# Two pre-activation convolutions by row transforms: an image's last outer products into their own slot, layer 2's statistics one slot earlier

## The chip, the cores and the metric

The kernel runs on one core of a Trainium2 chip. The metric is the device time of one execution in microseconds (us); of several executions the median is given. Below, TensorE is PE in the profile, VectorE is DVE, ScalarE is ACT, GpSimd is POOL, and SyncE is SP. A "q" behind an engine's name (SPq) marks its instructions that issue transfers. All data are float32. Time before: 1962.35 us, the median of three executions (1960.58 to 1964.09).

## What is computed

```python
# x: (8, 32, 252, 252); two weights: (32, 32, 5, 5)
def _gn(v, G=16, eps=1e-5):
    B_, C_, H_, W_ = v.shape
    g = v.reshape(B_, G, C_ // G, H_, W_)
    m = jnp.mean(g, axis=(2, 3, 4), keepdims=True)
    s = jnp.var(g, axis=(2, 3, 4), keepdims=True)
    return ((g - m) / jnp.sqrt(s + eps)).reshape(v.shape)

x = x + _L0_conv_ref(_gn(x), L0_conv_weight)    # 5x5, padded by reflection, written with FFTs
x = x + _L1_conv_ref(_gn(x), L1_conv_weight)
```

Each layer normalises every image in 16 groups of two channels over all its pixels, convolves it with a 5x5 filter whose border is reflected, and adds the input. A layer's normalisation needs sums over the whole image, so layer 2 of an image can't start before the last row of its layer 1 has its sums.

## The kernel before

**Layout.** 32 channels, the parity of a row and the parity of a column together fill the 128 partitions; so an image is 126 x 126 positions, and the 5x5 filter becomes a 3x3 one between 128-wide vectors. The normalisation is put into the weights (the scale) and into a bias (the mean), and the addition of the input into the weights too, by an identity block. In the code layer 1 has `l = 0` and layer 2 `l = 1`.

**Tiling.** Both layers cut each image into eight chunks `c` of 16 rows (four tiles `t` of four output rows). Rows are transformed so that four output rows take six products, called points 0 to 5, each of three matmuls (one per column of the filter) of 504 or 508 columns. VectorE makes the transformed inputs: row differences `v` (L544, and L546 for the last rows, which need the next chunk), quad terms `u12` (L554 to L557), then `t24` for points 2 and 4 (L565, L569), `t13` for 1 and 3 (L575, L572), `t05` for 0 and 5 (L582).

**A slot** is one chunk of one layer. The list `order` alternates layer 1 of image b+1 with layer 2 of image b; the first eight slots are layer 1 of image 0, the last eight layer 2 of image 7. In a slot TensorE computes points 2 and 4 into the banks `m2` and `m4`. ScalarE copies each into `pairs1` and `pairs3` as a "seed" (L691, L693) on which points 1 and 3 are then accumulated, and keeps a copy in `sd` (L699). VectorE combines them into the two middle output rows (L710, L718, L719).

The "outer" points 0 and 5, which make rows 0 and 3 of each tile, come in one of three ways:

- late (the usual one): in the following slot, accumulated on sums in the bank pair `sums05`, which ScalarE reads out (L734);
- by columns (`by_columns`): smaller products on column sums `sdiff`, `d`, half in the own slot in `extra` with a seed by ScalarE (L674), the rest in the next in `sums05`, read out by L746;
- at once (the set `at_once`): in the own slot, into `extra`, added and read out by VectorE (`outer`, L732).

**Statistics.** Reading out also gives row sums; ScalarE squares each finished chunk of layer 1 (`squares`, L818). When chunk 7 is in, `finish_stats` runs a chain for layer 2: `moments` on VectorE (`tot`, `mv`, `dk`, `nvar`), `group_mean` (a small matmul, L337), `deviations` (VectorE), `group_var` (a small matmul, L358), `variance` (VectorE's `var`, L364, then ScalarE's root `std`, L366), `inverse` (VectorE, to `rstd`). Then ScalarE scales the weights `u` (L506) and GpSimd adds the identity blocks (L474). The weights come from a copy in device memory (`ud`), written once by ScalarE's queue and fetched for each image by SP. Layer 1's own statistics of the next image are sums over 14 pieces `st` of x, read by SP and summed on ScalarE (L228, L230, L234).

For the early chunks of images 0 and 1, x is loaded only once and the second half of the partitions is made on the chip: GpSimd fills borders (L145 to L148) and ScalarE copies the even columns (`even_columns`, L156).

**What sets the order.** Nothing is scheduled by a planner: each operation is put into a table with a planned time by `at(t, fn, ...)`, the table is sorted, and every engine executes its own instructions in that order. The planned times decide the order alone; what waits in practice is decided by semaphores. `begin(i)` is the planned start of slot i. `t0`, `t1`, `t2` are the starts of a slot and of the next two. SP's transfers stand in one line in the same way.

The end of image b's layer 1 and the start of its layer 2, with the slots (b, l, c) = (b, 0, 7), (b-1, 1, 7), (b+1, 0, 0), (b, 1, 0), is called the boundary of image b below.

Of the kernel before, what the change touches and what calls it, by code (L numbers as in the profile page):

```python
# [42 lines left out]
ALU = mybir.AluOpType  # L43
# [10 lines left out]
def tile_conv_preact_x2(ctx: ExitStack, tc: tile.TileContext, x: bass.AP, w0: bass.AP, w1: bass.AP, out: bass.AP):  # L54
# [34 lines left out]
    def at(t: float, fn, *args, **kw):  # L89
        table.append((t, len(table), fn, args, kw))  # L90
# [437 lines left out]
    def transform(t0: float, t1: float, b: int, l: int, c: int, free: float = -100.0, now=(0, 0, 0)):  # L528
# [10 lines left out]
        def row_pairs(j0: int = 0, j1: int = NT):  # L539
            if j0 == 0:  # L540
                got["v"] = vpool.tile([P, ROWS, wi], F32, tag="v", name=f"v_{b}_{l}_{c}")
            v, (t, nxt) = got["v"], source()
            r0, r1 = 4 * j0, min(4 * j1, ROWS - 2)
            V.tensor_sub(v[:, r0:r1], t[:, r0 + 2 : r1 + 2], t[:, r0:r1])  # L544
            if j1 == NT:
                V.tensor_sub(v[:, r1:ROWS], nxt[:, 0:2], t[:, r1:ROWS])  # L546
            got["vt"] = v.rearrange("p (t i) w -> p t i w", i=4)

        def row_quads(j0: int = 0, j1: int = NT):
            if j0 == 0:  # L550
                got["u"] = vpool.tile([P, 2, NT, wi], F32, tag="u12", name=f"u12_{b}_{l}_{c}")
            u1, u2, (t, nxt) = got["u"][:, 0], got["u"][:, 1], source()
            r0, k1 = 4 * j0, min(j1, NT - 1)
            stt(u1[:, j0:j1], t[:, r0 + 1 : 4 * j1 : 4], -4.0, t[:, r0 + 3 : 4 * j1 : 4], ALU.mult, ALU.add)  # L554
            stt(u2[:, j0:k1], t[:, r0 + 2 : 4 * k1 : 4], -4.0, t[:, r0 + 4 : 4 * k1 + 1 : 4], ALU.mult, ALU.add)
            if j1 == NT:
                stt(u2[:, k1], t[:, ROWS - 2], -4.0, nxt[:, 0], ALU.mult, ALU.add)  # L557

        def point2(j0: int = 0, j1: int = NT):
            if j0 == 0:  # L560
# [43 lines left out]
        if (b, l, c) == order[0]:  # L604
            at(t0 - 33.3, row_quads, 0, 2)
            at(t0 - 31, point2, 0, 2)
            for fn in (row_pairs, point4):
                at(t0, fn, 0, 2)
            for fn in (row_quads, point2, row_pairs, point4):
                at(t0 + 0.2, fn, 2, 4)  # L610
            at(t0 + 4.9, point1)
            at(t0 + 5.5, point3)
            at(t0 + 6.2, points05)
        else:
            for dt, fn in ((0, row_pairs), (2, row_quads), (3.6, point2), (4.2, point4)):
                at(t0 + dt, fn)
            at(max(t0 + 5.5, free + 7.8), point1)
            at(max(t0 + 5.6, free + (11.1 if by_columns(*now) else 10.25)), point3)
            at(t1, points05)
            if by_columns(b, l, c):  # L620
                at(t1 + 1.5, columns)


    def conv(b: int, l: int, c: int, t0: float, t1: float, t2: float = 0.0, j0: int = 0, j1: int = NT, m05=None, later: float = 10.2):
# [130 lines left out]
            V.tensor_sub(half(sums05, 1, both, no), odd, m12[:, :, :, 0:no])  # L755

        step = 2.55 * f
        for i, k in enumerate((2, 4, 1, 3)):
            for h in range(3):
                if first and i < 2:  # L760
                    for j in (0, 2):
                        at(t0 + 1.3 * i + step * j / 2 + 0.1 * h, product, k, h, j, j + 2)
                else:
                    at(t0 + step * (i + h / 3) + (0.85 if columns and i == 3 and h else 0.0), product, k, h)
        for i, k in enumerate(() if columns else (0, 5)):
            for h in range(3):
                at((t1 - 2 * step if m05 else t1 + later) + step * (i + h / 3), product, k, h)
        for e in range(2):
            t = t0 + (5.1 * f if e else 3.9 if first else 2.6 * f)
            at(t, seed, e)  # L770
# [5 lines left out]
        if columns:  # L776
            for i in range(4):
                at(t0 + (11.05 if i % 2 else 8.5) + 0.2 * i, column_product, 2 - i % 2, i // 2)
                at(t1 + later + 0.4 * i, column_product, 3 * (i % 2), i // 2)
            at(t0 + 9.3, seed_columns)  # L780
            at(t0 + 12.9, parts05)
            at(t1 + 1.5, column_parts)
            for i in range(2):
                at(t2 + 0.05, outer_columns, i)
        elif m05:
            at(t0 + 12.9 * f, parts05)
            if (b, c) == (0, NCH - 1) or (l == 1 and nt == NT):
                at(t1 - 0.01, open_rest)
            at(t1, outer, 0)
            at(t1, outer, 1)  # L790
        else:
            at(t1 + 1.5, parts05)
            at(t2 + 0.05, outer, 0)
            at(t2 + 0.05, outer, 1)
        if nt < NT:
            store_half(t1, b, c, j0 // 2, got)
        elif l == 0:
            keep(t1, None if m05 else t2, b, c, got)
        else:
            store(t1 + 1.5 if m05 else t2 + 0.7, b, c, got)  # L800


    def keep(t1: float, t2, b: int, c: int, got):
# [33 lines left out]
            at(t1 + (0.4 if t2 is None else 2.0), shift)  # L837
        last = c == NCH - 1
        if t2 is None:
            times = t1 + 0.5, t1 + (8.7 if last else 13.4), t1 + 6.6  # L840
        else:
            times = t1 + 13.5, t2 + (0.7 if last else 9.7), t2 + 7.8
        if (b, c) == (0, 0):
            times = t1 + 5.9, *times[1:]
        at(times[0], squares, 0, slice(0, NT), slice(1, 3))
# [67 lines left out]

    at_once = {order.index(n) for n in [(0, 0, c) for c in range(NCH)] + [(0, 1, 0), (B - 2, 1, NCH - 3)]}

    def by_columns(b: int, l: int, c: int) -> bool:
        if l == 0:
# [6 lines left out]
    def begin(i: int) -> float:  # L926

        return sum(10.2 + (own + [0.0])[j] + (late[j - 1] if j else 0.0) for j in range(i))


    chained = {order.index((b, 0, NCH - 1)) + 2 for b in range(B)}


    t0 = -100.0
# [53 lines left out]
    for i, (b, l, c) in enumerate(order):  # L988
# [9 lines left out]
        else:  # L998
            conv(b, l, c, t0, t1, t2, later=10.2 + own[i + 1])
        if i + 1 < len(order):  # L1000
            transform(t0 + (6.3 if i == 0 else 3.5 if i in chained else 2.9), t1 + 0.2, *order[i + 1], free=t0, now=(b, l, c))
            nb, nl, ncx = order[i + 1]
            k = inputs.index((nb, ncx)) + 2
            if nl == 0 and 2 < k < len(inputs):
                for part in parts(*inputs[k]):
                    at(t0 + (14.0 if nb == 0 and part[0] == ROWS else 4.0), load, *inputs[k], *part)
                    at(t1 + 0.2, borders, *inputs[k], *part)
                    if once(*inputs[k]):
                        at(t1 + (0.3 if part[0] == 0 else 8.5), even_columns, *inputs[k], *part)
        if c == 0 and any(by_columns(b, l, k) for k in range(NCH)):  # L1010
            t = begin(i - 1) if l == 0 and b > 1 else t1 if l == 0 else t0
            at(t + 5.4, halve_middle, b, l)
# [4 lines left out]
        if l == 0 and b + 1 < B:  # L1017
            wide = 1 if b == 0 else 2
            if c == 0:
                for j in range(2):  # L1020
                    at(begin(i - 1 if b > 1 else i) + 1.0, load_piece, b + 1, j)
            if c < NPIECE // 2:
                for j in range(2):
                    p = 2 * c + j
                    t = (t1 if wide == 2 and j else t0) + (8.6 + 2.5 * j if wide == 1 else 9.8)
                    at(t, piece_sums, b + 1, p)
                    if p + 2 < NPIECE:
                        at(t + 2.6, load_piece, b + 1, p + 2)
# [5 lines left out]
                    at(t0 + (9.5, 10.4, 11.3)[j], scale_points, b + 1, 0, ks)  # L1034
                    at(t0 + (10.4, 12.3, 14)[j], lambda b=b, ks=ks: add_residual(G, scaled[b + 1, 0], ks))
        if l == 0 and c == NCH - 1:
            at(t2 + 0.1, fetch_weights, b, 1)
            finish_stats(b, 1, *(t2 + t for t in (1.45 if b else 0.1, 3.41, 3.42, 6.85, 7.0, 7.6)))
            for j, ks in enumerate(pairs):
                at(t2 + (9.5, 10.4, 13.6)[j], scale_points, b, 1, ks)  # L1040
                at(t2 + (10.4, 12.4, 14.5)[j], lambda b=b, ks=ks: add_residual(G, scaled[b, 1], ks))

    with tc.manual_schedule(engines={E.PE, E.DVE, E.Activation, E.Pool, E.SP}):
        for _, _, fn, args, kw in sorted(table, key=lambda e: e[:2]):
# [33 lines left out]
```

## Time and profile before

| | |
|---|---|
| median of three executions | 1962.35 us (1960.58 to 1964.09) |
| the profiled execution | 1960.66 us |
| its span, first to last instruction | 1958.9 us |
| TensorE busy, mean granted clock | 1894.1 us (97%), 0.988 |
| VectorE busy | 1749.5 us (89%) |
| ScalarE busy | 1400.0 us (71%) |
| GpSimd busy | 235.9 us (12%) |
| moved by DMA | 276.09 MB, 141 GB/s on average |

The page gives each engine's busy time, the chain of work that ended last, and the costliest groups. The table of waits gives, for one engine, the instruction that waited, what released it, the total, how often and the longest. A timeline gives single instructions (or runs of equal ones): start, duration, engine, line, operation, output and input, how many records, and in brackets the idle time before them with what ended it. A matmul of 504 columns has two records. The windows give the busy time of each engine in a stretch, the granted clock of TensorE, and the DMA's share.

### The profile page before, as it was taken

Reading aid. Unit: us, or ns where it says so; the run is one execution under the profiler, and the core shown is the slowest. Engines: PE = TensorE matmul, PEld = TensorE weight load, DVE = VectorE, ACT = ScalarE, POOL = GpSimd, SP = SyncE. Lnnn points to the kernel's source line nnn. Section 1 sums busy time; section 2 is a strip of 40 time slices with the busy share of each in tenths; the row PEclk is TensorE's granted clock in tenths of the full one; section 3 lists DMA queues with packets and bytes.
Section 4 is the critical chain, followed back from the end, with each engine's and each line's share of the span. In section 5 each row is a group of like instructions: output and inputs, shape, how many; then the busy total and the mean of one; then the engine's idle time right before and its main releaser. Section 6 shows DMA issues by size and latency. Waiting matters only on the chain.

```text
span 1958.9 us, 19376 instructions
## 1 busy us (share of the span) xinstructions
PE 1894.1 (97%) x5068; PEld 947.7 (48%) x5068; DVE 1749.5 (89%) x2924; ACT 1400.0 (71%) x2703; POOL 235.9 (12%) x541
## 2 busy tenths in 40 slices
PE   5999999999999999999999999999999999999998
PEld 4444444444544444544544444444454445444445
DVE  7978899899989999989989999989989999988896
ACT  5866677777777777777777687776877765665575
POOL 3542000110001100011000210002000020000100
PEclk8999999999999999999999999999999999999999
DMA  9875465757765766756856757666767636541133
GB/s 271 202 163 148 107 156 141 160 125 171 163 142 126 167 157 146 168 122 151 182 131 141 168 120 182 138 144 149 149 161 165 139 88 124 113 100 50 41 78 89
DMA packets 220974, 276.09 MB, mean 141 GB/s; under 512 B 16448, under 2 KB 204224, under 8 KB 218688
## 3 DMA queue, kind: packets, MB, share of 16 engines
q1 hardware_dynamic: 220384, 272.09, 61.5%
q10 hardware_dynamic: 480, 2.77, 0.4%
q8 instruction: 40, 0.66, 0.2%
q14 instruction: 70, 0.57, 0.1%
HBM read 207.41 MB, written 67.39 MB: 140 GB/s over the span
## 4 chain that ended last, share of the span: by engine, by line
PE 87%; DVE 5%; ACT 3%; DMA 3%; POOL 1%; issue 1%; SPq 0%; ACTq 0%; POOLq 0%; DVEq 0%
PE pairs L648 31%; PE m L648 30%; PE sums L648 15%; PE sums L670 5%; PE extra L670 5%; PE extra L648 2%; DMA st<-in_x_dram 1%; DVE v L544 1%; POOL u L474 1%; DMA xs<-in_x_dram 1%; ACT junk L818 1%; DMA wraw<-in_L_conv_weight_dram 0%; ACT y L734 0%; DVE d L595 0%; ACT u L506 0%
## 5 line engine op out<-in xcount | busy, mean ns | idle before, releaser
L648 PE MATMUL pairs<-t,u 128*128 128x504 f32 (+2 forms) x1548 | 690.5, 587 | 7.9 <-ACT pairs L691 4.5
L648 PE MATMUL m<-t,u 128*128 128x508 f32 (+3 forms) x1560 | 679.2, 583 | 5.0 <-POOL u L474 2.5
L648 PEld LDWEIGHTS pairs<-t,u 128*128 128x128 f32 x1548 | 291.4, 190 | 341.6 <-issue 322.9
L648 PEld LDWEIGHTS m<-t,u 128*128 128x128 f32 x1560 | 294.5, 190 | 330.3 <-issue 315.3
L875 ACT COPY o<-y 64x508 f32<-64x508 f32 x496 | 326.6, 659 | 9.4 <-DVE y L732 1.0
L648 PE MATMUL sums<-t,u 128*128 128x508 f32 (+3 forms) x732 | 314.8, 577 | 0.0
L734 ACT ACTIVATE y<-sums 128x508 f32<-128x508 f32 (+2 forms) x120 | 64.6, 583 | 218.7 <-PE sums L648 218.7
L582 DVE SCALAR_TENSOR_TENSOR t<-v 128x1024 f32<-128x1024 f32 (+1 forms) x128 | 157.8, 1233 | 60.8 <-PE sums L648 60.1
L648 PEld LDWEIGHTS sums<-t,u 128*128 128x128 f32 x732 | 137.8, 189 | 146.0 <-issue 139.0
L710 DVE SCALAR_TENSOR_TENSOR sd<-sd,pairs 128x504 f32<-128x504 f32 (+2 forms) x258 | 166.8, 672 | 43.1 <-PE pairs L648 41.2
L145 POOL COPY xs<-xs 64x32 f32<-64x32 f32 (+3 forms) x74 | 38.7, 523 | 1115.9 <-DMA xs<-in_x_dram 811.2
L699 ACT COPY sd<-m 128x504 f32<-128x504 f32 (+2 forms) x258 | 149.9, 581 | 1.5
L818 ACT ACTIVATE junk<-y,negk 128x1008 bf16<-128x1008 f32 x144 | 148.3, 1030 | 2.5
L706 ACT COPY sd<-pairs 128x504 f32<-128x504 f32 (+1 forms) x129 | 74.1, 574 | 88.2 <-PE pairs L648 84.2
L670 PE MATMUL extra<-sdiff,wc 128*128 128x252 f32 (+2 forms) x456 | 115.6, 375 | 20.8 <-ACT extra L674 20.8
L544 DVE TENSOR_TENSOR v<-xs 128x1792 f32<-128x1792 f32 (+1 forms) x65 | 129.9, 1999 | 0.7
L544 DVE TENSOR_TENSOR v<-y 128x1806 f32<-128x1806 f32 x64 | 130.0, 2031 | 0.0
L693 ACT COPY pairs<-m 128x504 f32<-128x504 f32 (+1 forms) x129 | 72.8, 564 | 75.0 <-PE m L648 73.3
L670 PEld LDWEIGHTS extra<-sdiff,wc 128*128 128x128 f32 x456 | 85.5, 190 | 82.3 <-issue 48.4
L234 ACT ACTIVATE st<-st,negk 128x1134 f32<-128x1134 f32 x98 | 121.7, 1242 | 3.3
L228 ACT ACTIVATE st<-st 128x1134 f32<-128x1134 f32 x98 | 112.0, 1143 | 4.4 <-DMA st<-in_x_dram 3.3
L670 PE MATMUL sums<-d,u 128*128 128x252 f32 (+2 forms) x456 | 108.4, 380 | 0.0
(172 smaller groups left out, 2221.9 us busy)
## 6 DMA issues: line engine op xcount, KB each, us to landing
xs<-in_x_dram SPq DMA_DIRECT2D x176, 504.0 KB, 8.5
st<-in_x_dram SPq DMA_DIRECT2D x111, 567.0 KB, 4.4
out_dram<-o SPq DMA_DIRECT2D x488, 126.0 KB, 6.7
u<-ud SPq DMA_DIRECT2D x15, 1152.0 KB, 6.1
xs<-in_x_dram SPq DMA_DIRECT2D x30, 441.0 KB, 6.8
xs<-in_x_dram SPq DMA_DIRECT2D x28, 472.5 KB, 8.3
ud<-uraw ACTq DMA_DIRECT2D x2, 1152.0 KB, 7.5
xtail<-in_x_dram SPq DMA_DIRECT2D x64, 31.5 KB, 6.4
```

The costliest lines, as they stand in the source:

```text
L228: A.activation(junk, src, AF.Identity, accum_out=acc[:, 0, i : i + 1])
L234: A.activation(junk, src, AF.Square, bias=negk, accum_out=acc[:, 1, i : i + 1])
L544: V.tensor_sub(v[:, r0:r1], t[:, r0 + 2 : r1 + 2], t[:, r0:r1])
L582: stt(t, got["vt"][:, :, 0:2], -4.0, got["vt"][:, :, 2:4], ALU.mult, ALU.add)
L648: T.matmul(dst, u[:, k, 2 - i, :], rhs[:, j0 + i0 : j0 + i1, i : i + wo], start=(i == 0 and not add), stop=(i == 2), skip_group_check=add,)
L670: T.matmul(dst[:, 0, use], w, rhs[:, use], start=(i == 2), stop=True, skip_group_check=(i != 2))
L693: A.copy(dst, src)
L699: A.copy(got["sd"][:, 1 + e], m24[e][:, 0:n])
L706: A.copy(got["sd"][:, 0], pairs13[0][:, 0:n])
L710: stt(d, d, -2.0, pairs13[e][:, 0:n], ALU.mult, ALU.add)
L818: A.activation(dst, src, AF.Square, bias=negk, accum_out=acc[:, 1, at_ : at_ + 1])
L875: copy(got["o", h][halves[s], 0:m, cp::2], got["y"][halves[cp], r : r + m, :])
```

## The change

- The last chunk of layer 1 of images 1 to 7, (b, 0, 7), joins the set `at_once`; image 0's was in it already. Its outer products go into `extra` in its own slot and are read out by VectorE. `open_rest` (one small identity matmul on the rest of `extra`) now follows in each of these slots.
- In such a slot the own outer products come directly after the inner ones, ahead of the late ones of the slot before: they are placed by `te`, which is `t0 + 6 * step`, and no more by the start of the next slot.
- Layer 2's chain of statistics, the fetch of its weights, their scaling and their residual are placed from `te = t0 + 15.3`, where they were placed from `t2`, two slots on. The squares of chunk 7 are placed earlier, its reflection copies later (`te + 22`).
- `last_rows` takes the last rows of `v` and `u12`, which need the next chunk, out of `row_pairs` and `row_quads`, and stands after both.
- The copies of even columns of the first two rows of a chunk come at `t1 + 5.25` instead of `t1 + 0.3`; both parts of (1, 0) at other times too.
- The first two loads of pieces of image 2, and the sums of the first piece, come later; the set `chained`, which put one transform per image 0.6 later, goes.

```diff
         def row_pairs(j0: int = 0, j1: int = NT):
...
             V.tensor_sub(v[:, r0:r1], t[:, r0 + 2 : r1 + 2], t[:, r0:r1])
-            if j1 == NT:
-                V.tensor_sub(v[:, r1:ROWS], nxt[:, 0:2], t[:, r1:ROWS])
...
         def row_quads(j0: int = 0, j1: int = NT):
...
-            if j1 == NT:
-                stt(u2[:, k1], t[:, ROWS - 2], -4.0, nxt[:, 0], ALU.mult, ALU.add)
+
+        def last_rows():
+
+            v, u2, (t, nxt) = got["v"], got["u"][:, 1], source()
+            V.tensor_sub(v[:, ROWS - 2 : ROWS], nxt[:, 0:2], t[:, ROWS - 2 : ROWS])
+            stt(u2[:, NT - 1], t[:, ROWS - 2], -4.0, nxt[:, 0], ALU.mult, ALU.add)
...
-            for dt, fn in ((0, row_pairs), (2, row_quads), (3.6, point2), (4.2, point4)):
+            for dt, fn in ((0, row_pairs), (2, row_quads), (3.2, last_rows), (3.6, point2), (4.2, point4)):
                 at(t0 + dt, fn)
...
         step = 2.55 * f
+        te = t0 + 6 * step if nt == NT else t1
...
-                at((t1 - 2 * step if m05 else t1 + later) + step * (i + h / 3), product, k, h)
+                at((te - 2 * step if m05 else t1 + later) + step * (i + h / 3), product, k, h)
...
         elif m05:
             at(t0 + 12.9 * f, parts05)
-            if (b, c) == (0, NCH - 1) or (l == 1 and nt == NT):
-                at(t1 - 0.01, open_rest)
-            at(t1, outer, 0)
-            at(t1, outer, 1)
+            if c == NCH - 1 if l == 0 else nt == NT:
+                at(te - 0.01, open_rest)
+            at(te, outer, 0)
+            at(te, outer, 1)
...
-            keep(t1, None if m05 else t2, b, c, got)
+            keep(te if m05 else t1, None if m05 else t2, b, c, got)
...
         if t2 is None:
-            times = t1 + 0.5, t1 + (8.7 if last else 13.4), t1 + 6.6
+            times = (t1 - 1.9, t1 + 1.6, t1 + 22) if last else (t1 + 0.5, t1 + 13.4, t1 + 6.6)
         else:
-            times = t1 + 13.5, t2 + (0.7 if last else 9.7), t2 + 7.8
+            times = t1 + 13.5, t2 + (0.7 if b == B - 1 and c == NCH - 2 else 9.7), t2 + 7.8
...
-    at_once = {order.index(n) for n in [(0, 0, c) for c in range(NCH)] + [(0, 1, 0), (B - 2, 1, NCH - 3)]}
+    at_once = {order.index(n) for n in [(0, 0, c) for c in range(NCH)] + [(b, 0, NCH - 1) for b in range(B)] + [(0, 1, 0), (B - 2, 1, NCH - 3)]}
...
-    chained = {order.index((b, 0, NCH - 1)) + 2 for b in range(B)}
...
-            transform(t0 + (6.3 if i == 0 else 3.5 if i in chained else 2.9), t1 + 0.2, *order[i + 1], free=t0, now=(b, l, c))
+            transform(t0 + (6.3 if i == 0 else 2.9), t1 + 0.2, *order[i + 1], free=t0, now=(b, l, c))
...
                     if once(*inputs[k]):
-                        at(t1 + (0.3 if part[0] == 0 else 8.5), even_columns, *inputs[k], *part)
+                        kb, kc = inputs[k]
+                        t = 5.25 if part[0] == 0 and (kb, kc) != (1, 0) else 13.55 if kb else 8.5
+                        at(t1 + t, even_columns, *inputs[k], *part)
...
             if c == 0:
                 for j in range(2):
-                    at(begin(i - 1 if b > 1 else i) + 1.0, load_piece, b + 1, j)
+                    at(begin(i - 1) + 1.0 if b > 1 else t0 + (8.0 if b else 1.0), load_piece, b + 1, j)
             if c < NPIECE // 2:
                 for j in range(2):
                     p = 2 * c + j
-                    t = (t1 if wide == 2 and j else t0) + (8.6 + 2.5 * j if wide == 1 else 9.8)
+                    t = (t1 if wide == 2 and j else t0) + (8.6 + 2.5 * j if wide == 1 else 14.5 if (b, p) == (1, 0) else 9.8)
                     at(t, piece_sums, b + 1, p)
...
         if l == 0 and c == NCH - 1:
-            at(t2 + 0.1, fetch_weights, b, 1)
-            finish_stats(b, 1, *(t2 + t for t in (1.45 if b else 0.1, 3.41, 3.42, 6.85, 7.0, 7.6)))
+            te = t0 + 15.3
+            at(te + 0.1, fetch_weights, b, 1)
+            finish_stats(b, 1, *(te + t for t in (3.0 if b < B - 1 else 4.4, 6.85, 6.86, 10.25 if b else 9.9, 12.82, 13.55)))
             for j, ks in enumerate(pairs):
-                at(t2 + (9.5, 10.4, 13.6)[j], scale_points, b, 1, ks)
-                at(t2 + (10.4, 12.4, 14.5)[j], lambda b=b, ks=ks: add_residual(G, scaled[b, 1], ks))
+                at(te + (14.5, 15.5, 21)[j], scale_points, b, 1, ks)
+                at(te + (15.5, 17.5, 22)[j], lambda b=b, ks=ks: add_residual(G, scaled[b, 1], ks))
```

## The prediction

> **What bounds the kernel now.** I read the page first, for busy shares and the chain that ended last, and then the table of TensorE's waits.
>
> ```profile
> PE 1894.1 (97%) x5068; PEld 947.7 (48%) x5068; DVE 1749.5 (89%) x2924; ACT 1400.0 (71%) x2703; POOL 235.9 (12%) x541
> ...
> PE 87%; DVE 5%; ACT 3%; DMA 3%; POOL 1%; issue 1%; SPq 0%; ACTq 0%; POOLq 0%; DVEq 0%
> ```
> ```profile
> PE extra L670 <- ACT extra L674: 20.8, 7, 3.0
> ...
> PE pairs L648 <- ACT pairs L691: 4.5, 4, 3.1
> PE m L358 <- DVE sq L352: 3.8, 6, 0.6
> PE pairs L648 <- issue: 3.3, 1, 3.3
> PE m L648 <- POOL u L474: 2.5, 3, 0.8
> ```
>
> TensorE sets the time. No matmul is removed, so only its waits can be won. They sum to 55.8 us; 19.7 lie in the start (the statistics' first load, 14.9, and five small ones). The other 36.1 are spread: 20.8 are seven waits of 3.0, one per image, for ScalarE's seed of `extra`; the rest stand beside them or in image 0. Half-speed stretches follow: six, at 136.7, 174.3, 658.9, 894.5, 1604.4 and 1822.9 us. Summing what matmuls took above their steady spacing (0.845 for 504 columns) over each boundary gives 14.1 in image 0 (100 to 300 us) and 5.3, 5.8, 5.8, 5.4, 5.3, 4.9, 5.2 in images 1 to 7. In all about 46, of which 10 is the clock.
>
> Next the timelines around image 1's boundary: ScalarE, VectorE, TensorE.
>
> ```profile
> 412.05 0.59 ACT L699 COPY sd<-m 128x504 f32<-128x504 f32 x1
> 418.33 0.20 ACT L366 ACTIVATE std<-var 128x1 f32<-128x1 f32 x1 [5.70 <-DVE var L364]
> ...
> 420.85 0.56 ACT L674 ACTIVATE extra<-extra 128x504 f32<-128x504 f32 x1
> ```
> ```profile
> 414.58 2.04 DVE L544 TENSOR_TENSOR v<-y 128x1806 f32<-128x1806 f32 x1
> ...
> 418.15 0.15 DVE L364 TENSOR_SCALAR var<-m 128x1 f32<-128x1 f32 x1
> ```
> ```profile
> 421.47 1.01 PE L670 MATMUL extra<-sdiff,wc 128*128 128x189 f32 x4 [2.98 <-ACT extra L674]
> ```
>
> ScalarE stands 5.70 us before the square root of layer 2's variance, since VectorE does 3.6 us of `v` and `u12` before `var`. Behind the root queue a copy, eight reflection copies (2.1) and the seed, which TensorE wants at 418.5. So the chain of statistics, placed in the slot in which `extra` is needed, makes the stall.
>
> The same engine's windows show what is left to win from:
>
> ```profile
> 411.90:427.20 15.30, 10.86 (x36) 5.91 (x35) 14.40 (x31) 9.42 (x23) 4.16 (x9) 1.00 0.43 133
> ...
> 442.50:457.80 15.30, 15.30 (x42) 7.53 (x41) 15.16 (x25) 10.66 (x24) 1.32 (x2) 1.00 0.66 169
> ```
>
> The columns are length, then PE, PEld, DVE, ACT and POOL. VectorE is busy 14.40 of the 15.30 in which TensorE stalls, and 15.16 two slots later. It has hardly any slack there.
>
> Image 0 has stalls of another kind (ScalarE, then SP's DMA issues):
>
> ```profile
> 172.48 0.42 ACT L156 COPY xs<-xs 64x256 f32<-64x256 f32 x1 [6.46 <-POOL xs L148]
> ...
> 174.06 0.63 ACT L691 ACTIVATE pairs<-m,means 128x504 f32<-128x504 f32 x1
> ```
> ```profile
> 160.52 0.94 SPq L247 DMA_DIRECT2D st<-in_x_dram  x2
> 174.70 2.02 SPq L140 DMA_DIRECT2D xs<-in_x_dram  x4
> 176.83 0.47 SPq L467 DMA_DIRECT2D u<-ud  x1
> ```
>
> A copy of even columns, waiting 6.46 for GpSimd's borders, stands before the seed; TensorE idles 3.26 until 174.79. The same happens at 137.71 (3.13).
>
> [...] The stretches here begin right after waits of 3.0 to 3.3, and granted clock in the slice at 656.7 to 672.0 is 0.89, some 1.7 us lost in 15.3. At images 1, 4 and 5 the same wait is followed by no such stretch, but by the 0.8 for GpSimd's `u`, so it depends on phase. [...] In 158 to 173 us 469 GB/s is the most the trace shows, and about 190 while strided image rows load (178 to 184).
>
> **The change part by part, images 1 to 6.** I walked image 1 (slot (1,0,7) starts at 373.99 in both).
>
> 1. Outer products of chunk 7: six matmuls (3 x 0.845 + 3 x 0.634 = 4.44) move one slot forward. TensorE's sum: 0, plus one identity matmul (about 0.14, the price of the small ones before). They end at 389.2 and the identity at 389.4. ScalarE loses two evacuations (0.59 + 0.48), VectorE gains two (0.60 + 0.48).
> 2. The chain. On VectorE: outer ends 390.8; `tot` waits for ScalarE's last squares until 391.9 (idle 1.15), `nvar` 392.8. Then `t05` (1.2) and the column forms (2.5) to 396.6; `mean` waits for TensorE's small matmul, 397.4 (0.8 idle). `v` and its followers for (2,0,0) take to 402.5, `var` 403.2. ScalarE's root follows; the seed of `extra` is ready at about 405.5 where TensorE wants it at 405.8: the 2.98, the 0.64, the 0.82 and the clock go, 5.3 to 5.8. What hides the wait for `var` is 0.3 us of slack; if `var` is later, the seed is late by as much.
> 3. What is late next. VectorE has done 1.1 us more and idled 2, so its lead grows by one us only. After `rstd` (406.1) it has 9.8 of differences, sums and outer rows, then `v` of (1,1,0) at 415.9 and 4.2 for `t24`: ready 420.1, wanted at 419.65, since TensorE comes 4 us sooner. I get stalls of 0.5 there, 1.0 at (2,0,1) and 0.5 a slot on, 2.0 to 2.2 with the identity. Gain per boundary 5.4 - 2.1 = 3.3; six make 19.8. From both sides: 5.4 if VectorE is never late, 1 if it is late by one us more in each of two slots.
> 4. Later squares, reflection and weights: the reflection copies (2.1) leave the critical stretch; they are read more than ten slots on, and ScalarE has 4 us of slack a slot (71% busy). The fetch of `u` moves a slot ahead on SP, past the statistics' loads of image b+2; it waits for the buffer until about 389, and those loads are issued there instead of at 382, wanted at 416: nothing. GpSimd's adds move with it, ready by 415, wanted at 425.
> 5. `last_rows`: same instructions, reordered by under 0.4 us inside one VectorE stretch: 0.
>
> **Image 7.** The root (5.13 of waiting before 1819.64) moves ahead of the first seed of (6,1,7), which TensorE wants at 1813.4; with `var` at 1812.3, the root, a copy and then the seed make about 1816. The stall is 2.7 for 5.2: gain 2.5, from 0 to 5.
>
> **Image 0.** The even-column copies now follow both seeds, so the waits at 137.7 and 174.8 and their clock losses go (about 9.8); the copies' own cover is the next transform, about 6 us off. But the changed order of ScalarE has, between the first and second seed of (1,0,1): the root, an even-column copy (1.82), the first scaling of `u_0_1` (0.94), and the sums of `st_2_0` (1.31 + 0.20 + 1.43). TensorE wants that second seed at 178. On SP, `st_2_0` stood ahead of the rest (160.52 above); now it is behind the fetch of `u_0_1` and four loads of `xs_1_3`. The fetch waits for ScalarE's write of `ud1`, issued about 162.7, 8 to 10 us in landing: 171. Then 1.2 + 2.1 + 0.6 MB: at about 400 GB/s for the whole rows and 190 for the strided, 3 + 11 + 1.5 us, landing at 187. Seed at about 190, a stall of 12 with 1.7 of clock. (0,1,0) then starts near 198, and started at 197.8. Net 0: without a late load the seed would come at 183 and 7 be won; at 194, 4 lost. Start and end of the kernel: 0.
>
> **Sum.** 19.8 + 2.5 + 0 = 22.3. The profiled execution took 1960.66 (span 1958.9): 1938.4. The median is 1.7 above it, at 1962.35, so 1940.
>
> **The rivals.**
>
> - VectorE keeps up (13 in 100). The stalls of step 3 don't come: 6 x 5.3 + 4, and 0 to 5 of image 0: 36 to 41, 1921 to 1926. For it: TensorE's table has only 0.6 of waits for `t`, and none after the start. Against: 15.16 of 15.30.
> - VectorE becomes the bound for longer (19 in 100). Its debt isn't paid back for several slots because it starts each with under 1 us of slack; about 1.5 kept per boundary, 2 of images 0 and 7: 11, so 1951.
> - Slower (6 in 100): the square root on ScalarE, in the new place, blocks the seeds as at image 0 and 7. Nothing but 0.3 us covers it. Price: each us by which `var` comes after 403.2 + 0.3 is a us of TensorE, and past a stall of 3 the clock takes 1.7. It decides at `var` near 406.8 (3.3 gone into the stall); at 408, 4.5 + 1.7 against 3.3 is 2.9 lost per boundary, 17 over six, and with image 0 losing 4: about 1979; just past the point, 1967.
> - The change does nothing of what it says (4 in 100): the seed is released late by something else, such as ScalarE's squares, and stalls just move: 1958 to 1966.
>
> **How the numbers follow.** My forecast has 58 in 100, with its own range 1931 to 1949 (1 us either way per boundary, 4 in image 0). To hold 8 in 10 I take part of each neighbour: 1925 to 1954; outside remain half of the first rival, the slower one and the idle one, with the forecast's tails. Within 0.2% (3.9 us) is about what measuring can't tell from no change: 4 in 100, slower 6, faster 90.
>
> **What would show it.** Right: the wait `extra <- ACT extra L674` falls from 20.8 to about 3 and `sq` and `u L474` vanish; TensorE shows new waits for VectorE's `t` of 0.5 to 1 in two or three slots after each boundary; a stall of about 12 at 178 us on the second seed in image 0, released by ScalarE behind a wait for `st`; one of 2.7 near 1813. Wrong: no waits for `t` (the first rival), or ScalarE's root waiting past 406 (the third). What would upset the sum most is image 0's load, and a VectorE debt that I have undercounted by 1 us, which counts six times.

## The result, and the profile after

The changed kernel takes 1943.4 us (median of four executions, 1942.39 to 1943.66) beside 1961.46 for the kernel before on the same chip (1960.41 to 1964.09): a ratio of 0.9905, 95% interval 0.9888 to 0.9922. That is 18 us less. The forecast was 1940, with a range of 1925 to 1954. The profiled execution took 1943.66, its span is 1941.9 (before: 1958.9).

The page's busy times and the chain that ended last:

```profile
PE 1887.5 (97%) x5082; PEld 941.9 (49%) x5082; DVE 1759.6 (91%) x2952; ACT 1396.4 (72%) x2675; POOL 254.7 (13%) x541
...
PE 80%; DVE 14%; DMA 3%; issue 1%; ACT 1%; SPq 0%; DVEq 0%; ACTq 0%
```

TensorE is still the bound, but VectorE's share of the chain rose from 5% to 14% and ScalarE's fell from 3% to 1%. VectorE took over 10 us of work and GpSimd's busy time rose by 19 us with the same 541 instructions; both come up again below.

TensorE's table of waits (what waited, what released it, total, how often, longest):

```profile
PE pairs L653 <- ACT pairs L698: 7.0, 1, 7.0
PE m L653 <- DVE t L567: 6.9, 7, 1.0
PE m L653 <- issue: 3.4, 3, 1.1
PE m L653 <- POOL u L474: 3.0, 3, 1.0
PE m L653 <- DVE var L364: 3.0, 1, 3.0
```

The seven waits of 3.0 for the seed of `extra` are gone. There are four kinds in their place: one of 7.0 in image 0, two of about 1 at every boundary (the first is named three times "issue" and three times `u L474`, the second `t L567`), and one of 3.0 in image 7. Under whichever name, each of the six first waits ends 0.1 after VectorE's L567 does (shown for image 1 below: 415.75 + 0.70, and TensorE at 416.54), so they too are waits for `t`.

A stretch at half rate, below, is one in which the trace's granted clock is 0.50: between its start and its end the kernel before has six, the changed kernel two, from 182.2 in image 0 and from 1796.7 in image 7, and none at the boundaries of images 1 to 6. To see what each wait is worth I cut both traces at TensorE's first product of three slots:

| stretch | before | after | gain |
|---|---|---|---|
| to (0,0,1) | 52.79 | 52.13 | 0.7 |
| image 0, to (0,1,1) | 166.43 | 162.44 | 4.0 |
| six boundaries, to (6,1,1) | 1417.23 | 1404.96 | 12.3, or 2.04 each |
| image 7 and the end | 322.42 | 322.35 | 0.1 |

So the forecast sum of 19.8 + 2.5 + 0 became 12.3 + 0.1 + 4.0, with 0.7 of the start, which no part of the change explains and which varies by more (51.6 to 53.5) between the runs below. These are stretches of one execution each. The kernel before varies most: beside the runs below its executions took 1955.5 to 1965.8, so its stretches may lie some us off those of another execution.

TensorE at image 1's boundary in the changed kernel, as a timeline:

```profile
416.54 5.35 PE L653 MATMUL m<-t,u 128*128 128x508 f32 x12 [1.12 <-issue]
...
429.51 5.34 PE L653 MATMUL m<-t,u 128*128 128x504 f32 x12 [1.01 <-DVE t L567]
...
438.75 1.12 PE L675 MATMUL extra<-sdiff,wc 128*128 128x252 f32 x4 [0.17 <-DVE sdiff L594]
```

The two windows of the same stretch (length, then PE, PEld, DVE, ACT, POOL busy):

```profile
411.90:427.20 15.30, 14.18 (x43) 7.39 (x42) 15.16 (x23) 12.14 (x23) 5.73 (x8) 1.00 0.16 46
427.20:442.50 15.30, 14.04 (x40) 7.02 (x39) 15.02 (x24) 11.81 (x32) 0.58 (x2) 1.00 0.93 180
```

VectorE, busy 14.40 of the 15.30 before in the first of these windows, is now at 15.16 and 15.02. TensorE waits on it three times in 22 us, by 1.12, 1.01 and 0.17; the fourth pause, 0.09 at 437.47, is for a seed. These are the waits that step 3 of the prediction expected (0.5, 1.0 and 0.5).

### The profile page after: what moved, and what is told of

The parts are those of the page before. It is cut to its first block, busy times and chain, and to the rows that moved or that the text cites. A ratio compares the mean times of both kernels' runs of the same rounds, so it can differ in the third digit from the quotient of the medians.

```text
span 1941.9 us, 19423 instructions
## 1 busy us (share of the span) xinstructions
PE 1887.5 (97%) x5082; PEld 941.9 (49%) x5082; DVE 1759.6 (91%) x2952; ACT 1396.4 (72%) x2675; POOL 254.7 (13%) x541
## 4 chain that ended last, share of the span: by engine, by line
PE 80%; DVE 14%; DMA 3%; issue 1%; ACT 1%; SPq 0%; DVEq 0%; ACTq 0%
PE m L653 27%; PE pairs L653 27%; PE sums L653 14%; PE extra L675 4%; PE extra L653 4%; PE sums L675 4%; DMA st<-in_x_dram 2%; DVE v L544 2%; DVE sd L715 1%; DVE t L584 1%; DVE t L577 1%; DVE y L723 1%; DVE y L724 1%; DVE u L552 1%; DVE t L574 1%
## 5 line engine op out<-in xcount | busy, mean ns | idle before, releaser
L653 PE MATMUL sums<-t,u 128*128 128x508 f32 (+3 forms) x648 | 281.4, 582 | 0.0
L715 DVE SCALAR_TENSOR_TENSOR sd<-sd,pairs 128x504 f32<-128x504 f32 (+2 forms) x258 | 165.9, 670 | 41.5 <-PE pairs L653 38.5
L739 ACT ACTIVATE y<-sums 128x508 f32<-128x508 f32 (+2 forms) x106 | 57.2, 590 | 200.9 <-PE sums L653 200.9
L653 PEld LDWEIGHTS sums<-t,u 128*128 128x128 f32 x648 | 121.0, 188 | 128.5 <-issue 125.3
L824 ACT ACTIVATE junk<-y,negk 128x1008 bf16<-128x1008 f32 (+1 forms) x144 | 148.3, 1030 | 8.8 <-DVE y L724 5.7
L544 DVE TENSOR_TENSOR v<-xs 128x1792 f32<-128x1792 f32 (+1 forms) x65 | 130.3, 2005 | 1.8 <-issue 1.1
L698 ACT COPY pairs<-m 128x504 f32<-128x504 f32 (+1 forms) x129 | 72.6, 563 | 81.7 <-PE m L653 62.5
L544 DVE TENSOR_TENSOR v<-y 128x1806 f32<-128x1806 f32 x64 | 130.2, 2034 | 0.0
L474 POOL TENSOR_TENSOR u<-u,resid 32x64 f32<-32x64 f32 x180 | 92.3, 513 | 215.2 <-ACT u L506 204.8
```

The source lines that it names most:

```text
L474: eng.tensor_add(dst, dst, resid[quad(cp, rp), ks])
L653: T.matmul(dst, u[:, k, 2 - i, :], rhs[:, j0 + i0 : j0 + i1, i : i + wo], start=(i == 0 and not add), stop=(i == 2), skip_group_check=add,)
L715: stt(d, d, -2.0, pairs13[e][:, 0:n], ALU.mult, ALU.add)
L824: A.activation(dst, src, AF.Square, bias=negk, accum_out=acc[:, 1, at_ : at_ + 1])
```

## The experiments

All are edits of the changed kernel. Beside the medians, the stretches of the table above are compared, since they leave out the start. In the runs that don't touch a stretch it repeats: 1404.5 to 1405.3 for the six boundaries, 161.2 to 163.0 for image 0, and 322.2 to 322.5 for the last one (once 320.8, see the end).

**The chain's place, alone undone.**

```diff
         if l == 0 and c == NCH - 1:
+            if 0 < b < B - 1:
+                at(t2 + 0.1, fetch_weights, b, 1)
+                finish_stats(b, 1, *(t2 + t for t in (1.45, 3.41, 3.42, 6.85, 7.0, 7.6)))
...
+                continue
```

> The changed kernel with layer 2's chain of statistics, its weights, scaling and residual of images 1 to 6 back at their old place two slots on; the outer products stay in their own slot. Theory: the place of the chain makes the stall (the root before the seed of the column products), and the outer products alone win nothing: each boundary loses what the change won there (2.1) and somewhat more, since VectorE does the outer rows on top: 12 to 18 us slower than the changed kernel, 1956 to 1962. Rival: having the outer rows earlier is what helps, and the chain's place is secondary: at most 5 us slower, under 1949.

1959.94, ratio 0.9994 (0.9986 to 1.0003): the whole gain is gone. The boundaries take 1422.55, that is 17.6 more than in the changed kernel and 5.3 more than before. The outer products in their own slot, with all the rest of the change, win nothing at the boundaries without the early chain: together they cost 0.9 each there. They pay by letting the chain start earlier. What I had put wrongly is the wait's name. This kernel's largest wait of TensorE is

```profile
PE m L358 <- DVE sq L352: 20.0, 6, 3.3
```

It is the small matmul of the chain itself (`group_var`) that stands in TensorE's order and waits for VectorE, not the seed behind ScalarE's root: the chain's place makes the stall, by whichever of its links is late first. Each of these waits of 3.3 is followed by a stretch at half rate; the mean granted clock is 0.986, beside 0.992 in the changed kernel.

The other half, late outer products with the early chain, wasn't tried: the chain would then sum rows that aren't made yet.

**GpSimd's additions out of VectorE's way.** First what they do. VectorE in the changed kernel, at the transform of (1,1,0):

```profile
413.44 0.81 DVE L552 SCALAR_TENSOR_TENSOR u<-y 128x516 f32<-128x516 f32 x1
414.17 0.67 DVE L553 SCALAR_TENSOR_TENSOR u<-y 128x387 f32<-128x387 f32 x1
414.77 0.54 DVE L558 TENSOR_TENSOR v<-y,y 128x258 f32<-128x258 f32 x1
415.23 0.41 DVE L559 SCALAR_TENSOR_TENSOR u<-y,y 128x129 f32<-128x129 f32 x1
415.75 0.70 DVE L567 TENSOR_TENSOR t<-u 128x516 f32<-128x516 f32 x1
```

and GpSimd:

```profile
384.39 3.00 POOL L474 TENSOR_TENSOR u<-u,resid 32x64 f32<-32x64 f32 x7
...
411.70 6.38 POOL L474 TENSOR_TENSOR u<-u,resid 32x64 f32<-32x64 f32 x8
```

The first four took 0.69, 0.56, 0.42 and 0.29 in the kernel before (416.53 to 418.23): each is 0.12 longer here. And GpSimd's additions took 0.43 each, pauses included, at 384 and 0.80 at 411.7.

```diff
-                at(te + (14.5, 15.5, 21)[j], scale_points, b, 1, ks)
-                at(te + (15.5, 17.5, 22)[j], lambda b=b, ks=ks: add_residual(G, scaled[b, 1], ks))
+                at(te + (14.5, 15.5, 16.0 if 0 < b < B - 1 else 21)[j], scale_points, b, 1, ks)
+                at(te + ((15.5, 16.5, 17.0) if 0 < b < B - 1 else (15.5, 17.5, 22))[j], lambda b=b, ks=ks: add_residual(G, scaled[b, 1], ks))
```

> The changed kernel with GpSimd's second and third groups of residual additions of images 1 to 6 put right behind the first, ahead of the borders that wait for a load (and ScalarE's third scaling next to the second). Theory: at 411.7 to 418.1 these additions [...]slow seven of them by about 0.12 each, so that the input of (1,1,0) is 0.6 to 0.8 late; at 405 to 409 VectorE mostly reads one operand from PSUM and isn't slowed. The first wait at each boundary falls from about 1.1 to 0.4 and the second from 1.0 to about 0.5: 5 to 7 us less than the changed kernel over six boundaries, about 1937. Rival: the wait is VectorE's own load of work and the additions slow it wherever they stand: within 1.5 us of the changed kernel.

1940.36, ratio 0.9903 (0.9886 to 0.9919); 3 less by the medians, which the intervals alone would not tell apart. The boundaries do: 1401.45, 3.5 less than the changed kernel, 0.58 each. VectorE at the same place, with the additions ended at 409.4:

```profile
413.72 0.68 DVE L552 SCALAR_TENSOR_TENSOR u<-y 128x516 f32<-128x516 f32 x1
414.33 0.55 DVE L553 SCALAR_TENSOR_TENSOR u<-y 128x387 f32<-128x387 f32 x1
414.80 0.41 DVE L558 TENSOR_TENSOR v<-y,y 128x258 f32<-128x258 f32 x1
415.14 0.28 DVE L559 SCALAR_TENSOR_TENSOR u<-y,y 128x129 f32<-128x129 f32 x1
```

The first wait fell from 1.12 to 0.61 and the second from 1.01 to 0.82. The theory holds at half the size that I expected. Six instructions of this transform were longer, not seven: five by 0.12 and L577 by 0.06. The four above have both inputs in SBUF, and each was 0.12 longer beside the additions. In this run the additions (402.83 to 409.39) stood mostly beside instructions with one input in PSUM instead: L729 at 406.07 kept its 0.67. L574 at 404.08, with both in SBUF, took 0.81 beside them, and 0.69 at 419.79 without.

**Less work for VectorE.** The expectation says what is left out.

```diff
-            at(t + 8.2, column_weights, b, l)
+            if l == 1 or b < 2:
+                at(t + 8.2, column_weights, b, l)
```

> The changed kernel without VectorE's three operations on the column weights of layer 1 for images 2 to 7 (1.26 us, at 398.6 for image 2), so that the products by columns use the weights of image 1; all other work stays. Theory: after the change VectorE's lack of lead is what is left of each boundary's stall. Taking 1.26 us from it before the transform of (1,1,0) removes the first wait there (1.1) nearly whole and leaves the second (1.0), as TensorE then comes sooner too: 1.2 us per boundary, 7 us over six, 1936. Rival: the wait is set by something else that ends last (GpSimd's additions, which the waits name at three boundaries): within 1.5 us of the changed kernel.

1939.58, ratio 0.9898 (0.988 to 0.9915). The boundaries take 1401.10, 3.9 less, 0.64 each: neither 1.2 nor nothing. 1.26 us were taken from VectorE and half came back. VectorE's timeline says where the other half went:

```profile
400.36 0.68 DVE L715 SCALAR_TENSOR_TENSOR sd<-sd,pairs 128x508 f32<-128x508 f32 x1
401.67 0.68 DVE L715 SCALAR_TENSOR_TENSOR sd<-sd,pairs 128x508 f32<-128x508 f32 x1 [0.64 <-PE pairs L653]
```

VectorE now reaches the second difference before TensorE has made its `pairs` and waits 0.64 for them. From there it works almost without a pause to 415.93, where the input of (1,1,0) is ready; TensorE needs that at 415.52 (416.03 less its 0.51 of waiting). So VectorE is the limit in a loop: TensorE's product, a stretch of 14.3 of VectorE's work, TensorE's next. Part of a saving ahead of the loop's start is lost in waiting for TensorE; one inside it counts, as GpSimd's additions did. That is read from these two runs; one with both savings was not made.

**Image 0.** ScalarE in the changed kernel, between the two seeds of (1,0,1) (L696, L698):

```profile
175.10 0.20 ACT L366 ACTIVATE std<-var 128x1 f32<-128x1 f32 x1 [1.70 <-DVE var L364]
...
175.79 1.84 ACT L156 COPY xs<-xs 64x1792 f32<-64x1792 f32 x1
177.90 0.94 ACT L506 ACTIVATE u<-u,rstd 128x768 f32<-128x768 f32 x1 [0.26 <-DVE rstd L378]
181.40 1.15 ACT L228 ACTIVATE st<-st 128x1134 f32<-128x1134 f32 x1 [2.56 <-DMA st<-in_x_dram]
...
184.15 0.57 ACT L698 COPY pairs<-m 128x504 f32<-128x504 f32 x1
```

That is the order that the prediction walked, with the wait for the load in it. Two runs test what it costs and what the copies win.

```diff
-                    t = (t1 if wide == 2 and j else t0) + (8.6 + 2.5 * j if wide == 1 else 14.5 if (b, p) == (1, 0) else 9.8)
+                    t = (t1 if wide == 2 and j else t0) + (8.6 + 2.5 * j if wide == 1 else 16.0 if (b, p) == (1, 0) else 9.8)
```

> The changed kernel with one time altered: in image 0 the sums of the first statistics piece of image 2 stand behind both seeds of (1,0,1) on ScalarE, no longer between them. Theory: the 7.00 us wait of TensorE at 184.77 for the second seed is the price of the load and the sums standing ahead of it (2.56 waiting for the load, 2.7 of sums), and the stretch at half rate behind it costs 1.7 more. The root (175.10), an even-column copy and the first scaling (to 178.8) still stand ahead, so a wait of about 1.3 remains and no stretch: 7 us less than the changed kernel, about 1936. Rival: the late load only moves the stall, since the next instruction of ScalarE's queue that TensorE needs is behind the same sums: within 2 us of the changed kernel.

1941.72, ratio 0.9909 (0.9895 to 0.9924), and image 0 takes 161.99 for 162.44, no clear difference. The rival was right. TensorE's timeline of this run:

```profile
178.74 2.80 PE L653 MATMUL pairs<-t,u 128*128 128x504 f32 x6 [1.60 <-ACT pairs L698]
...
195.59 5.16 PE L653 MATMUL pairs<-t,u 128*128 128x508 f32 x6 [4.49 <-ACT pairs L696]
```

The 7.00 fell to 1.60, near the 1.3 worked out, and the next slot's first seed took over 4.49 of it, with the stretch at half rate (5.16 for these six records, 2.80 for the six at 178.74). From 178.6 to 194.8 ScalarE works with hardly a pause: three pieces' sums, the scalings, eight reflection copies and squares all stand ahead of that seed.

```diff
-                        t = 5.25 if part[0] == 0 and (kb, kc) != (1, 0) else 13.55 if kb else 8.5
+                        t = 0.3 if part[0] == 0 else 8.5
```

> The changed kernel with the copies of even columns at their old times (ahead of ScalarE's seeds). Theory: what image 0 won comes from these copies: with them back, the waits of about 3.1 and 3.3 for seeds in image 0 and their stretches at half rate return, beside the new wait of 7.0 at 185: about 8 us slower than the changed kernel, 1951. Rival: the earlier chain of image 0 took the statistics' reads off GpSimd and the copies find their borders in time: within 2 us of the changed kernel.

1953.51, ratio 0.9959 (0.9945 to 0.9973). Image 0 takes 173.16, 10.7 more: TensorE waits 3.25 at 137.88, 3.34 at 173.87 and 4.27 at 194.50. So the copies' new place wins about 10; without it the rest of the change makes image 0 longer than before (173.16 beside 166.43).

The last rows by themselves can't be put back, since the row differences would then be made ahead of the later copies that they read. So both were put back:

> The changed kernel with both the copies of even columns at their old times and the last rows of the row differences back inside their functions; beside the run with the copies alone back (1953.5, ratio 0.9959) it prices the last rows alone. Theory: the split of the last rows moves work by under 0.4 us within one stretch of VectorE and is worth nothing by itself (it lets the last rows be made after the later copies): within 2 us of that run. Rival: VectorE is the limit at the boundaries, and the place of the variance relative to these rows tells: 3 us or more apart.

1952.56, ratio 0.9959 (0.9947 to 0.9972): the same as with the copies alone back, within the 4 us over which the executions of either run spread. (In the profiled ones image 0 takes 170.20 for 173.16, but the start is 1.5 longer.) A worth of the split by itself doesn't show; it is what allows the later copies.

**Image 7.** VectorE makes `var` at 1796.26, behind output rows and outer points, and TensorE's third product into `m2` waits 2.96 for it. Only one time was altered:

```diff
-            finish_stats(b, 1, *(te + t for t in (3.0 if b < B - 1 else 4.4, 6.85, 6.86, 10.25 if b else 9.9, 12.82, 13.55)))
+            finish_stats(b, 1, *(te + t for t in (3.0 if b < B - 1 else 4.4, 6.85, 6.86, 10.25 if b else 9.9, 12.82 if b < B - 1 else 10.9, 13.55)))
```

> The changed kernel with one time altered: in image 7 VectorE makes the variance right after the point-1 sum of (6,1,7), ahead of the differences, output rows and outer points behind which it stood. Theory: the variance comes at 1792.3 instead of 1796.3, before TensorE's third product into the bank m2 (1793.5) that waits for it, so the 2.96 wait at 1796.46 goes, and with it the stretch at half rate (7.7 us recorded, some 1.7 to 3.9 lost): 4.5 to 5 us less than the changed kernel, about 1938.5. Rival: as I predicted, it is ScalarE's root standing before the seed of (6,1,7) that blocks: then the same gain but the wait named would have been a seed; and a second rival: the root now waits elsewhere and TensorE stalls on VectorE's late rows instead: within 1.5 us of the changed kernel.

1941.83, ratio 0.9911 (0.9896 to 0.9925); the last stretch takes 322.39, just what it took. ScalarE's timeline:

```profile
1790.62 0.20 ACT L366 ACTIVATE std<-var 128x1 f32<-128x1 f32 x1 [1.91 <-DVE var L364]
1796.92 0.94 ACT L506 ACTIVATE u<-u,rstd 128x768 f32<-128x768 f32 x1 [6.09 <-DVE rstd L378]
1797.76 0.64 ACT L696 ACTIVATE pairs<-m,means 128x508 f32<-128x508 f32 x1
```

The wait for `var` is down to 0.53, and TensorE waits 2.43 for the seed (L696) instead, again with a stretch at half rate behind it (from 1798.15; each of the two lasts 3.4, not the 7.7 of the expectation). So my own mechanism, the chain's work on ScalarE ahead of that seed, was there, hidden behind another of the same length; it is the scaling of `u` that blocks, and no longer the root. With both mended, by placing that scaling behind the seed too:

```diff
-                at(te + (14.5, 15.5, 21)[j], scale_points, b, 1, ks)
+                at(te + ((14.5, 15.5, 21) if b < B - 1 else (14.8, 15.5, 21))[j], scale_points, b, 1, ks)
```

> The run with the sooner variance of image 7, and besides ScalarE's first scaling of layer 2's weights of image 7 put behind the first seed of (6,1,7) instead of ahead of it. Theory: two reasons stood one behind the other at this place. With the sooner variance the wait for it fell from 2.96 to 0.53, but the first seed of (6,1,7) then waited 2.43, since the scaling ahead of it on ScalarE waited 6.09 for VectorE's inverse. With both mended the waits at 1790 to 1798 sum to under 0.6 and no stretch at half rate follows: 4 us less than the changed kernel (about 1938 by the median, some 0.988 of the kernel before). Rival: a third thing is late behind these two (the weights of (7,1,0), or VectorE's rows): the gain stays at 1 to 2 us.

1940.4, ratio 0.9901 (0.9884 to 0.9919). The last stretch takes 318.96, 3.4 less; 0.53 and 0.63 of waiting are left and no stretch at half rate there (mean granted clock 0.993, 0.991 in the run without it).

**All mends together.** The additions, image 7's two times, and in image 0 the first scaling, the sums of the first and third piece and the reflection copies behind the seeds:

```diff
-            times = (t1 - 1.9, t1 + 1.6, t1 + 22) if last else (t1 + 0.5, t1 + 13.4, t1 + 6.6)
+            times = (t1 - 1.9, t1 + 1.6, t1 + (36 if b == 0 else 22)) if last else (t1 + 0.5, t1 + 13.4, t1 + 6.6)
...
+                    t += 13.2 if (b, p) == (1, 2) else 0.0
                     at(t, piece_sums, b + 1, p)
...
+                at(te + ((14.5, 15.5, 16.0) if 0 < b < B - 1 else (15.45, 15.5, 21) if b == 0 else (14.8, 15.5, 21))[j], scale_points, b, 1, ks)
```

> All the mends together: additions sooner, image 7's variance sooner and its scaling behind the seed, and in image 0 the first scaling, the sums of the first and third piece and the reflection copies moved behind the seeds that they delayed. Theory: additions 3.5 (measured alone), image 7 about 4, image 0 the wait of 7.0 and its stretch, some 8: 15 us less than the changed kernel, about 1928, 0.983 of the kernel before. Rival for image 0: ScalarE's debt of some 5 us is only passed on, as it was when the first sums alone were moved: 1935.

1928.33, ratio 0.9841 (0.9824 to 0.9858), 15 below the changed kernel and as forecast. Image 0 takes 154.11 (8.3 less), the boundaries 1401.58 (3.4), the last stretch 319.15 (3.2), and no stretch at half rate is left between the start and the end (mean granted clock 0.995). TensorE's waits after the start:

```profile
PE m L653 <- DVE t L567: 5.8, 7, 0.9
PE m L653 <- issue: 3.7, 6, 0.6
...
PE pairs L653 <- ACT pairs L698: 1.0, 2, 0.6
```

The stall of image 0 was thus not passed on for ever: it had to be spread over the slots in which ScalarE has room. What is left, 0.6 and 0.8 at each boundary, is VectorE's loop by the reading above.

## Why the prediction was right, and where its steps were not

**What bounds, and what the change does: right.** The stall of each boundary came from the place of the statistics' chain, and with it back in its old place the gain was gone (1959.94). The waits for the seed of `extra` fell from 20.8 to nothing that the table shows, and the half-rate stretches at the boundaries went too. The walk of step 2 held nearly to the tenth: counted from the start of (1,0,7), which is 369.25 in the trace and not 373.99, `var` was forecast at 29.2 and came at 29.3. `last_rows` showed no worth of its own, the end 0, `u`'s fetch past the loads of later pieces showed no wait.

**Step 3, the gain per boundary: mis-sized by 1.3.** I took 5.4 before less 2.1 after, 3.3; it was 2.04. The three waits that I worked out for image 1 (2.0 in all) sum to 2.30 in the trace, so the walk itself held. What failed is that 5.4 was TensorE's time above steady spacing, which holds more than idle time, while 2.1 was idle time (with the identity matmul). In the trace of after the same measure gives 3.4 at the four pauses of image 1: where the table shows 1.12 of idle, the product comes 1.28 later than its spacing, and the next is late by another 0.1. With 5.4 against 3.4 the step would have said 2.0, and six of these 12; the sum would have been 1948. Idle time on both sides says the same for image 1: 0.64 + 2.98 + 0.82 before, less 2.39 after, is 2.05. Of the first wait, 0.5 of its 1.12 was GpSimd's additions, which step 4 put at no cost since they would be ready in time: they were, but I hadn't asked beside which VectorE instructions they would fall.

**Image 7: right in place, mis-sized.** The stall was forecast at 2.7 and is 2.96, but the gain is 0.1 and not 2.5. The same mistake: 5.2 before held the stretch at half rate, and the 2.7 after left out that a stretch follows again (it does, at 1796.7); by the same measure the boundary has 5.0 after. And the wait that ends last is one for `var` by TensorE itself, which I hadn't seen; the one that I had named stood right behind it.

**Image 0: right order, load too late.** I had the seed at 190 and a stall of 12; it came at 184.15, a stall of 7.00 with its stretch, so 4.0 were won for a forecast of 0. The failing term is the fetch of `u_0_1`, put at 171: ScalarE issued the write of `ud1` at 158.7, not 162.7, and SP could issue the fetch at 162.9, 4 us after the write and not 8 to 10. The load of `st_2_0` was there at 181.4 instead of 187. The range that I gave for this (7 won, 4 lost) holds it. By the forecast's own slope, 7 won at 183 and nothing at 190, a seed at 184.15 should have won nearly 6; why it was about 2 less stays open, and the stretch repeats only within 1.8.

**The rivals.** That VectorE keeps up fell: it is busy 15.16 of 15.30. That it stays the bound for several slots fell too: from (1,1,1), at 447.4, TensorE waits no more until the next boundary. The slower one did not come: with `var` at 398.6 and the seed at 400.3, ScalarE was ahead of TensorE (401.3). The mistakes of the terms were 7.5 too much at the boundaries, 2.4 too much in image 7 and 4.0 too little in image 0, so in the profiled execution 17.0 were won for 22.3. That the total came so near is in part luck, since the errors partly cancelled.

Two sums of the prediction don't come out, without effect on the forecast: the time above steady spacing is 52 and not 46 (image 7's 5.2 is missing), and the third rival at 408 with image 0's 4 is 1983 and not 1979.

## What to carry to other kernels

When a stall is traded for a smaller one, both sides must be measured in one unit: idle time against idle time, or time above steady spacing against the same, with what a pause adds (about 0.26 each here) and the slow clock on both sides. In an order written by hand, a wait that is removed shows the next in the same queue, so ask for every instruction between it and the work that TensorE needs, and move them together: one alone won nothing clear in image 7 or in image 0, all of them 3.2 and 8.3. Where VectorE is full, GpSimd's small operations weren't free here; they cost less beside VectorE's instructions that read PSUM (L729 kept its 0.67) than beside its row transform (L552 went from 0.69 to 0.81). And a stall's length alone didn't tell whether a stretch at half rate followed (one did after 2.96, none after 2.97); the next section has what did.

## What the runs showed of the hardware

- Some VectorE instructions and GpSimd's additions were longer beside each other. In the changed kernel an addition beside VectorE instructions that read PSUM (L715, L723) took 0.31; one that started during L544 (both inputs in SBUF, 411.48, 2.04 long) took 1.99 and ended 0.17 after it:

```profile
402.59 0.31 POOL L474 TENSOR_TENSOR u<-u,resid 32x64 f32<-32x64 f32 x1 [15.21 <-ACT u L506]
...
411.70 1.99 POOL L474 TENSOR_TENSOR u<-u,resid 32x64 f32<-32x64 f32 x1
```

  Five of the instructions that followed were 0.12 longer each, whatever their length (0.69 to 0.81, 0.29 to 0.41). L544 itself, which had started ahead of the additions, kept its 2.04, and L567, which started after a pause of 0.10, its 0.70. Over the changed kernel's trace after 60 us, the instructions that additions covered for over half of their time had these medians, beside those without any: L552 0.81 for 0.69, L553 0.67 for 0.55, L558 0.54 for 0.43, L559 0.40 for 0.28, L571 0.81 for 0.69, L577 0.81 for 0.75. L715, L723 and L729, which have an input in PSUM, were within 0.01 of theirs; but so were L567, L724 and L730, with both inputs in SBUF. So two inputs in SBUF alone don't tell which one is longer, and what does was not shown.
- The granted clock changed only on a grid of 3.413 us: in the traces before and after, all 24 stretches of one granted clock ahead of each trace's last, which the end cuts off, are whole multiples of it within 0.01, from 3.41 to 1607.68 (471 of them). In the changed kernel the clock changes at 189.02, 1796.70 and 1800.12, which are 471 steps and one step apart. Whether a stall was followed by a stretch at half rate went with how it lay on this grid. Image 7's stall of 2.96 in the changed kernel lies in one window of the grid; the stall of 2.97 at the same place in the run with image 0's first sums moved is split over two (the windows are those of the grid; the columns are as above, and the clock is the third from the end):

```profile
1793.29:1796.70 3.41, 0.45 (x2) 0.24 (x2) 3.41 (x7) 0.20 (x1) 0.00 (x0) 1.00 0.00 0
1796.70:1800.12 3.42, 3.42 (x5) 1.39 (x5) 3.25 (x10) 1.52 (x3) 0.45 (x2) 0.50 0.00 0
```
```profile
1790.98:1794.39 3.41, 1.81 (x5) 0.52 (x3) 3.41 (x6) 0.00 (x0) 0.00 (x0) 1.00 0.00 0
1794.39:1797.80 3.41, 2.03 (x5) 1.05 (x6) 3.24 (x11) 0.20 (x1) 0.00 (x0) 1.00 0.00 0
1797.80:1801.22 3.42, 3.41 (x8) 1.24 (x7) 3.42 (x6) 3.30 (x6) 2.09 (x4) 1.00 0.00 0
```

  TensorE is idle for 2.96 of the one window, and half rate follows; it is idle for 1.60 and 1.38 of the two, and none follows: the last stretch took 320.83 instead of 322.35. So nearly the same stall cost 1.5 more in one run than in the other. In the traces before and after, from 30 us on, each of the eight full-rate windows with 2.13 or more of TensorE's idle time was followed by one at half rate, and none with 1.52 or less was; of the four between, the one with 1.82 was, those with 1.86, 1.90 and 1.95 were not. The half-rate windows with 1.01 and 2.57 of idle time were each followed by another; the nine with 0.55 or less were not. In the kernel before, the 3.0 of images 1, 4 and 5 lie as 1.52 + 1.46, 1.95 + 1.02 and 1.11 + 1.86, and no stretch follows; those of images 2, 3, 6 and 7 have 2.31 to 2.98 in one window, and one does. So a window need not have been wholly idle: 2.13 of 3.41 was enough at 133.29 in the kernel before. The prediction's 1.7 "past a stall of 3" was my estimate from the waits of 3.0 to 3.3 that it names.
- Each of the four pauses of TensorE at image 1's boundary in the changed kernel cost about 0.16 us more than the idle time that the profile names, and the product after it another 0.1 (1.28 and 0.08 for the 1.12 at 416.54). The profile counts idle time from the end of the last record, and a record of 504 columns lasts 0.58 where the next one starts after 0.42 in steady work; the difference is the 0.16.
